# The first adjacency product of a two-layer graph kernel: begun on arriving quarters, three of its seven sub-products by an inner scheme, the transpositions and projections moved behind it

## The chip, the cores and the metric

The kernel runs on one core of one Trainium2 chip. The core has TensorE (PE; its weight loads are shown apart as PEld), VectorE (DVE), ScalarE (ACT), GpSimd (POOL) and SyncE (SP), which here only issues transfers to the core's 16 DMA engines. The metric is the device time of one execution in microseconds (us), the median over several. Everything is in 32-bit floating point.

## The reference

```
x: 16 x 1024 x 64    adj: 1024 x 1024
layer 0:  Q = x Wq' + bq;  K = x Wk' + bk;  V = x Wv'
          score = softmax(Q K', over the rows n)      # per batch, 1024 x 1024
          x = layernorm(x + (score @ adj) @ V)
layer 1:  x1 = adj @ x;  x2 = 2 adj @ x1 - x          # twice, with the same adj
          x = layernorm(x + [x, x1, x2, x1, x2] @ weight + bias)
```

The kernel multiplies adj by x first, U = adj @ x for all 16 batches at once (1024 x 1024 by 1024 x 1024), lets the softmax weights act on U, and applies Wv afterwards. Both layers together need three such products with adj: this first one, and two "hops" in layer 1.

## The kernel before

**Data.** `xs` holds x with 128 nodes on the partitions: 8 pairs of batches, 8 blocks of nodes, 128 columns (2 batches x 64). `aT` holds adj transposed, 8 blocks of 128 rows by 1024. `xT` is x with channels on the partitions (`transposed`, L104: eight 128x128 transposes into a PSUM tile, which ScalarE copies out). `GY` is x projected by one matrix made of both score weights (`project`, L127: two 128x512 matmuls, and VectorE adds the bias on the way out). `score_weight` and `score_weight_2` (L111, L118) make that matrix.

**A product with adj** (class `Product`, L245) is cut into quarters of 512 and done with seven sub-products instead of eight, named 1 to 7. It needs sums of quarters of adj (`left_sum`, S1 to S4) and of quarters of x (`right_sum`, T1 to T4), four VectorE instructions of 128x512 each; T2 and T4 overwrite T, T3 overwrites S1, and S3 overwrites a quarter of `aT`, which is loaded again later (L523). `step` (L334) is one half of a sub-product: eight 128x512 matmuls into a two-bank PSUM tile, then the read of that tile. A read of cells not touched before is a ScalarE copy; a read onto cells that hold something is a VectorE add (L308).

**The inner scheme** (`halves`, L339; `part`, L363) does one sub-product itself with seven parts of four 128x256 matmuls, 28 instead of 16 twice as wide. It takes eight more VectorE sums, four of each factor, placed in a spare buffer, and reads a 128x512 bank per part. Before the change only the two hops use it. `twice` names the sub-products that are treated so: their common term is then added where another step is read, so steps 5 and 7 are read into two places.

**Order.** The program is written out by hand and each engine follows its own order. Sums wait in a list, `line`: `later` appends, `fill(n)` issues the next n at that point of VectorE's order, `need` issues all up to a name.

**PSUM.** Of eight banks, six are three two-bank tiles that rotate (`ps_tile`), two are the accumulator (`pacc`).

**The start before** (L74 to L151). ScalarE issues the score weights' transfers, GpSimd the bias's, SP x by pairs and adj by rows of 1024, then the small weights. TensorE runs idle turns (matmuls of zeros), then interleaves eight transpositions and eight projections. Then (L491 to L528) comes the first product: all S sums and T1, `layer_weights` (small sums that prepare Wv and the second layer's weights), row sums `mu`, then all seven sub-products plain, the last half-step interleaved with the scores of two steps of the attention loop.

**The loop** (L537) has 64 steps, 8 pairs of batches by 8 blocks. In step n TensorE makes scores of step n+2 (two rotating tiles, one for each batch), then the weighted sum `acc` of step n (L437); VectorE negates the scores and takes their minimum (L407); ScalarE takes the exponentials (L414). From pair 1 on, steps also carry the layer norm, re-transposition and weights of the pair before. GpSimd subtracts the row means from `xs` (L526), which the layer norm needs in pair 1.

Of the kernel before, what the change touches and what calls it, by code (L numbers as in the profile page):

```python
# [9 lines left out]
FP = mybir.dt.float32  # L10
# [8 lines left out]
def gnn_kernel(  # L19
# [31 lines left out]
    def ps_tile(name):  # L51
        return ps.tile([P, 2 * H], FP, tag="ps", name=name)
# [18 lines left out]
    raw = const.tile([P, 5, C], FP, tag="raw", name="raw")  # L71
    w1s = const.tile([P, 5, C], FP, tag="w1s", name="w1s")
    halves = [slice(j * C, (j + 1) * C) for j in range(2)]
    for w, w_in in ((wq, wqT), (wk, wkT)):  # L74
        for s in halves:
            nc.scalar.dma_start(w[s, s], w_in)
    for s in halves:
        nc.gpsimd.dma_start(bkp[s], bk[:, None])
    for k in range(0, K8, 4):
        nc.sync.dma_start(xs[:, 0, k : k + 4], x_in[:, 0, k : k + 4])  # L80
    for p in range(1, NP):
        nc.sync.dma_start(xs[:, p], x_in[:, p])
    for k in (4, 5, 6, 7, 0, 1, 2, 3):
        nc.sync.dma_start(aT[:, k], a_in[:, k])
# [19 lines left out]
    def transposed(p, pt=None):  # L104

        pt = ps_tile("pt") if pt is None else pt
        for k in range(K8):
            nc.tensor.transpose(pt[:, ts(k, P)], xs[:, p, k, :], ident)  # L108
        nc.scalar.activation(xT[:, p], pt, AF.Copy)

    def score_weight():  # L111
        pw = ps_tile("pw")
# [3 lines left out]
        return pw  # L116

    def score_weight_2(pm):  # L118
        nc.tensor.matmul(pm[:, H : H + P], wn[:, 1], wn[:, 0], start=True, stop=True)
        nc.tensor.matmul(pm[:, 2 * H - P : 2 * H - P + 1], wn[:, 0], bkp, start=True, stop=True)  # L120
        nc.vector.tensor_copy(m_w, pm[:, H : H + P])
        nc.vector.tensor_copy(gb, pm[:, 2 * H - P : 2 * H - P + 1])

    def rows_of(p):
        return xs[:, p].rearrange("p k (b c) -> p (k b) c", b=2)

    def project(p):  # L127
        pg = ps_tile("pg")
        for h in range(2):
            nc.tensor.matmul(pg[:, ts(h, H)], m_w, xT[:, p, ts(h, H)], start=True, stop=True)  # L130
        nc.vector.tensor_scalar(GY[:, p], pg, gb, None, op0=ALU.add)

    def idle_turns(n):

        pt = pacc.tile([P, N], FP, tag="acc", name="idle")
        for _ in range(n):
            nc.tensor.matmul(pt[:, 0:P], still, still, start=True, stop=True)

    idle_turns(6)
    transposed(0)  # L140
    idle_turns(4)
    transposed(1)
    pm = score_weight()
    idle_turns(2)
    transposed(2)
    score_weight_2(pm)
    for p in range(NP):
        if p + 3 < NP:
            transposed(p + 3)
        project(p)  # L150

# [59 lines left out]
    def left_tiles():  # L211
        return {n: quarter_tile("e", f"S{n}", 3) for n in (2, 4, 1)}

# [13 lines left out]
    def by_pair(t):  # L227

        return t.rearrange("p k (q f) -> p q k f", f=P)
# [4 lines left out]
    def later(name, pieces):  # L234
        line.extend((name, piece) for piece in pieces)
# [5 lines left out]
    def need(*names):  # L241
        while any(name in names for name, _ in line):
            fill(1)

    class Product:  # L245
# [69 lines left out]
        def matmuls(self, name, g, rows=(0, 1)):  # L315
# [3 lines left out]
            for i in rows:  # L319
                for k in range(HB):  # L320
# [123 lines left out]
    def take(p):  # L444
        LN[p] = att.tile([P, N], FP, tag="rT", name="rT")
        nc.scalar.activation(LN[p], ACC.pop(p), AF.Copy)

    def norm_1(p, po=None):
# [18 lines left out]
    def weigh(p, c, pw=None):  # L467
# [20 lines left out]
            U[:, blocks, ts(p, P)].rearrange("p k (b c) -> p k b c", b=2), to[:, 1], AF.Copy  # L488
        )

    S = left_tiles()  # L491
    first = Product(
        S, xs, by_pair(U), [ps_tile("h0"), pacc.tile([P, N], FP, tag="acc", name="h1")]
        + [ps_tile(f"h{n}") for n in (2, 3)],
    )
    for n in (1, 2, 4, 3):
        later("S", left_sum(S, n))
    later("T", first.right_sum(1))
    need("S", "T")
    wv = layer_weights()  # L500
    for p in range(NP):
        nc.vector.tensor_reduce(mu[:, p], rows_of(p), AX.X, ALU.add)
    nc.vector.tensor_scalar(mu, mu, 1.0 / C, None, op0=ALU.mult)
    for name in (2, 1, 5):
        first.step(name, 0)
        first.step(name, 1)
    later("T", first.right_sum(2) + first.right_sum(3))
    need("T")
    first.step(3, 0)
    first.step(6, 0)  # L510
    first.step(6, 1)
    later("T", first.right_sum(4))
    need("T")
    first.step(7, 0)
    first.step(7, 1)
    first.step(3, 1)
    first.step(4, 0)
    for i in range(2):
        first.step(4, 1, 0, (i,))
        scores(i)  # L520
        for j in range(2):
            exponentials(i, j)
    nc.sync.dma_start(aT[:, low, right], a_in[:, low, right])  # L523
    scaled(0)
    for p in range(NP):
        nc.gpsimd.tensor_tensor(  # L526
            rows_of(p), rows_of(p), mu[:, p, :, None].to_broadcast([P, G, C]), ALU.subtract
        )  # L528


    Y = GY.rearrange("p q (k f) -> p q k f", k=K8)
# [4 lines left out]
    last = len(steps) - 1  # L536
    for n, (p, m) in enumerate(steps):  # L537
        if (p, m) == (NP - 2, 2):
            later("half", [f for both in zip(*hop_1.halves(2, room[0])) for f in both])
# [63 lines left out]
    def turns(product, room, after_5, after_6):  # L603

        S = product.S
        need("S1", "T1")
        lefts, rights = product.halves(3, room[0])
        later("half", [f for both in zip(lefts, rights) for f in both])
# [12 lines left out]
        need("S2", "T2")  # L621
        if after_5:
            later("S3", left_sum(S, 3))
        lefts, rights = product.halves(4, room[1])
        later("half", lefts)
        for g in range(2):
            product.step(6, g, 6)
            after_6(g)
        need("S3", "T3")
        later("T4", product.right_sum(4))  # L630
        later("half", rights)
        for g in range(2):
# [47 lines left out]
    later("half", [f for both in zip(lefts, rights) for f in both])  # L680
    hop_2.tiles = [h[0], h[2], h[3], h[1]]
    hop_2.step(1, 0, 9)
    hop_2.part(2, 1, two)
# [51 lines left out]
```

## Time and profile before

| quantity | value |
| --- | --- |
| time, median of 8 runs | 617.1 us (615.54 to 618.34) |
| time of the profiled execution | 617.47 us |
| its span, first to last instruction | 615.4 us |
| TensorE busy | 600.3 us (98%) |
| VectorE, ScalarE, GpSimd busy | 391.3, 225.5, 86.9 us |
| mean granted TensorE clock | 0.994 |
| first product begins, on TensorE | 32.19 us |
| weighted sum of the loop's step 0 begins | 135.74 us |
| read from HBM, written | 9.73 MB, 4.19 MB |

The profile shows one execution. A row gives start and length in us, the engine, the line of the kernel, the operation, output and inputs with their shapes, the number of instructions merged, and in brackets how long the engine had been idle and what ended that. One 32-bit matmul is two records, so counts of matmuls are twice the instructions, except for transposes. "PEclk" is the share of the full clock that TensorE was granted. In the slices each digit is a busy share in tenths.

### The profile page before, as it was taken

How to read it: one execution, taken by the hardware profiler on the slowest of the kernel's cores; microseconds unless marked ns; L12 is line 12 of the kernel's file. 1: busy time of each engine (PE TensorE's matmuls, PEld its weight loads, DVE VectorE, ACT ScalarE, POOL GpSimd, SP SyncE). 2: the span in 40 equal slices, each digit the busy share in tenths (PEclk: the TensorE clock that was granted, in tenths of full speed). 3: DMA queues.
4: the chain of work that ended last, by engine and by line, in shares of the span. 5: the costliest groups of instructions: out<-in, count | busy, mean ns of one | idle time of the engine just before them, and what ended most of it. 6: DMA issues, size and time to landing. Idle time of an engine off the chain costs nothing.

```text
span 615.4 us, 6249 instructions
## 1 busy us (share of the span) xinstructions
PE 600.3 (98%) x2414; PEld 294.3 (48%) x2414; DVE 391.3 (64%) x702; ACT 225.5 (37%) x377; POOL 86.9 (14%) x47
## 2 busy tenths in 40 slices
PE   7999999999999999999999999999999999999993
PEld 7544444433334444343444434447647466646463
DVE  0599312157776767777676787946768477558484
ACT  2300100055657767676676767662100000000111
POOL 1000004400030210303011030300000000203366
PEclk8999999999999999999999999999999999999998
DMA  7700000100000000000000000000000000000012
GB/s 289 277 0 2 0 0 0 69 0 0 2 2 0 1 0 1 2 1 1 1 0 1 1 1 1 0 1 0 2 0 1 0 0 1 0 35 35 34 70 102
DMA packets 7245, 14.32 MB, mean 23 GB/s; under 512 B 1968, under 2 KB 2992, under 8 KB 7216
## 3 DMA queue, kind: packets, MB, share of 16 engines
q1 hardware_dynamic: 6832, 13.86, 6.1%
q8 instruction: 19, 0.31, 0.2%
q10 hardware_dynamic: 320, 0.07, 0.1%
q14 instruction: 10, 0.08, 0.0%
q0 software_dynamic: 64, 0.00, 0.0%
HBM read 9.73 MB, written 4.19 MB: 23 GB/s over the span
## 4 chain that ended last, share of the span: by engine, by line
PE 92%; DVE 4%; ACT 1%; DMA 1%; issue 0%; ACTq 0%; DVEq 0%
PE h L321 33%; PE sc L400 20%; PE acc L437 19%; PE h L374 9%; PE pw L473 3%; PE po L452 2%; PE pg L130 2%; PE pt L108 2%; DMA wk<-in_wkT_dram 1%; DVE GY L308 1%; DVE U L308 1%; PE h L473 1%; DVE var L191 0%; DVE e L407 0%; DVE T L275 0%
## 5 line engine op out<-in xcount | busy, mean ns | idle before, releaser
L407 DVE TENSOR_SCALAR_CACHE_REDUCE e<-sc 128x1024 f32<-128x1024 f32 x128 | 151.6, 1222 | 64.3 <-PE sc L400 64.3
L414 ACT ACTIVATE e<-e,nm 128x1024 f32<-128x1024 f32 x128 | 146.3, 1143 | 75.3 <-DVE e L407 75.2
L400 PE MATMUL sc<-xT,GY 64*128 64x512 f32 x512 | 128.4, 615 | 0.5 <-DVE e L407 0.5
L437 PE MATMUL acc<-e,us 128*64 128x512 f32 x512 | 124.0, 605 | 0.3 <-DVE us L425 0.3
L184 POOL TENSOR_TENSOR rstd<-var,expo 128x16 f32<-128x16 f32 (+1 forms) x15 | 42.1, 2807 | 417.2 <-DVE var L179 417.2
L321 PE MATMUL h<-T,S 128*128 128x512 f32 x192 | 83.4, 592 | 0.0
L400 PEld LDWEIGHTS sc<-xT,GY 64*128 64x128 f32 x512 | 45.0, 186 | 73.4 <-issue 49.8
L308 DVE TENSOR_TENSOR U<-h,U 128x512 f32<-128x512 f32 (+1 forms) x39 | 36.1, 935 | 53.7 <-PE h L321 45.6
L437 PEld LDWEIGHTS acc<-e,us 128*64 128x64 f32 x512 | 31.0, 136 | 71.0 <-issue 60.6
L658 ACT ACTIVATE sq<-GY 128x1024 f32<-128x1024 f32 x6 | 6.3, 1058 | 147.9 <-DVE GY L308 147.9
L321 PEld LDWEIGHTS h<-T,S 128*128 128x128 f32 x192 | 36.5, 190 | 44.6 <-issue 44.2
L310 ACT ACTIVATE U<-h 128x1024 f32<-128x1024 f32 (+1 forms) x9 | 8.4, 930 | 91.4 <-PE h L321 91.4
L321 PE MATMUL h<-S,aT 128*128 128x512 f32 x96 | 41.7, 592 | 0.0
L374 PE MATMUL h<-xs 128*128 128x256 f32 x144 | 32.6, 382 | 1.4 <-DVE GY L308 1.1
L374 PEld LDWEIGHTS h<-xs 128*128 128x128 f32 x144 | 27.0, 190 | 6.2 <-DVE GY L308 1.5
L308 DVE TENSOR_TENSOR GY<-h,GY 128x512 f32<-128x512 f32 (+1 forms) x24 | 19.1, 797 | 16.7 <-PE h L321 11.2
L526 POOL TENSOR_TENSOR xs<-xs,mu 128x1024 f32<-128x1024 f32 x8 | 15.0, 1903 | 104.7 <-DVE T L275 92.3
L321 PEld LDWEIGHTS h<-S,aT 128*128 128x128 f32 x96 | 18.2, 190 | 23.0 <-issue 23.0
L321 PE MATMUL h<-xs,aT 128*128 128x512 f32 x64 | 27.6, 592 | 0.0
L473 PEld LDWEIGHTS pw<-raw,xT 64*128 64x128 f32 x224 | 19.2, 187 | 15.8 <-issue 5.8
L414 ACT ACTIVATION_READ_ACCUMULATOR e<-e,nm 128x1 f32 x128 | 24.0, 188 | 0.0
L473 PE MATMUL pw<-raw,xT 64*128 64x192 f32 x224 | 24.0, 332 | 0.0
(145 smaller groups left out, 584.0 us busy)
## 6 DMA issues: line engine op xcount, KB each, us to landing
aT<-in_adjT_dram SPq DMA_DIRECT2D x8, 512.0 KB, 10.2
xs<-in_x_dram SPq DMA_DIRECT2D x7, 512.0 KB, 7.9
out_dram<-GY SPq DMA_DIRECT2D x12, 256.0 KB, 2.3
aT<-in_adjT_dram SPq DMA_DIRECT2D x1, 1024.0 KB, 5.1
out_dram<-GY SPq DMA_DIRECT2D x8, 128.0 KB, 1.9
xs<-in_x_dram SPq DMA_DIRECT2D x2, 256.0 KB, 3.1
w1s<-in_w_dram SPq DMA_DIRECT2D x2, 80.0 KB, 9.2
wq<-in_wqT_dram ACTq DMA_DIRECT2D x2, 16.0 KB, 5.2
```

Of the source, the lines that this page charges most:

```text
L108: nc.tensor.transpose(pt[:, ts(k, P)], xs[:, p, k, :], ident)
L130: nc.tensor.matmul(pg[:, ts(h, H)], m_w, xT[:, p, ts(h, H)], start=True, stop=True)
L184: nc.gpsimd.tensor_tensor(rstd, var, expo[:, 0:g], ALU.pow)
L308: nc.vector.tensor_add(at(self.res), got, at(self.res))
L321: nc.tensor.matmul(pt[:, ts(i, H)], a[:, k, ts(2 * g + i, P)], b[:, :, k], start=(start and k == 0), stop=(k == HB - 1), skip_group_check= ...
L374: nc.tensor.matmul(pt[:, ts(i, W)], a[:, k, ts(i, P)], b[:, :, k], start=(start and i == k == 0), stop=(k == 1), skip_group_check=True,)
L400: nc.tensor.matmul(sc[j][:, ts(h, H)], GY[s, p, ts(m, P)], xT[s, p, ts(h, H)], start=True, stop=True,)
L407: nc.vector.tensor_scalar(E[n][:, j], sc[j], -1.0, None, op0=ALU.mult, op1=ALU.min, accum_out=NM[n][:, j : j + 1],)
L414: nc.scalar.activation(E[n][:, j], E[n][:, j], AF.Exp, bias=NM[n][:, j : j + 1], scale=-1.0, accum_out=SM[n][:, j : j + 1],)
L437: nc.tensor.matmul(ACC[p][j * C : (j + 1) * C, ts(h, H)], us[:, j], es[:, j, ts(h, H)], start=(m == 0), stop=(m == K8 - 1),)
L473: nc.tensor.matmul(pw[:, j, ts(k, 3 * C)], xT[s, p, ts(2 * c + k, P)], raw[s, 0:3].rearrange("p w c -> p (w c)"), start=True, stop=True,)
L526: nc.gpsimd.tensor_tensor(rows_of(p), rows_of(p), mu[:, p, :, None].to_broadcast([P, G, C]), ALU.subtract)
```

## The change

All transfers are now issued by SP. First come eight pairs: one node block of x for the first four batch pairs, and the left half of one row block of adj, 256 KB each. Then follow the other halves and the small weights.

The eight idle turns are followed at once by sub-product 1, block by block (`by_block`, new). Sub-products 2, 3 and 4 go by the inner scheme, with `GY`, which is empty as yet, as the spare buffer. In between stand the score weights, transpositions 0 to 3 and projections 0 to 3; these use the PSUM tiles of the product. Transposition 4 comes after the product, transpositions 5 to 7 and projections 4 to 7 stand in the loop's steps of pair 0. The bias of the projection is added by ScalarE. `layer_weights` comes after sub-product 7, the row sums `mu` are spread as fillers, and the means are subtracted in `centre`, five pairs before the loop and three in it.

```diff
+    for blocks in (range(K8 // 2), range(K8 // 2, K8)):
+        for k in blocks:
+            nc.sync.dma_start(xs[:, 0 : NP // 2, k], x_in[:, 0 : NP // 2, k])
+            nc.sync.dma_start(aT[:, k, 0:H], a_in[:, k, 0:H])
+    for p in range(NP // 2, NP):
+        nc.sync.dma_start(xs[:, p, 0 : K8 // 2], x_in[:, p, 0 : K8 // 2])
+    for k in range(K8):
+        nc.sync.dma_start(aT[:, k, H:N], a_in[:, k, H:N])
+    for p in range(NP // 2, NP):
+        nc.sync.dma_start(xs[:, p, K8 // 2 : K8], x_in[:, p, K8 // 2 : K8])
...
-        nc.vector.tensor_scalar(GY[:, p], pg, gb, None, op0=ALU.add)
+        nc.scalar.activation(GY[:, p], pg, AF.Identity, bias=gb, scale=1.0)
...
-    idle_turns(6)
-    transposed(0)
...
+    idle_turns(8)
...
+        def by_block(self, name):
+
+            a, b = self.factors(name)
+            for k in range(HB):
+                for i in range(HB):
+                    nc.tensor.matmul(
+                        self.tiles[i // 2][:, ts(i % 2, H)], a[:, k, ts(i, P)], b[:, :, k],
+                        start=(k == 0), stop=(k == HB - 1),
+                    )
...
+    h = [ps_tile("h0"), ps_tile("h1"), pacc.tile([P, N], FP, tag="acc", name="h2"), ps_tile("h3")]
+    two = h[2:]
+    first = Product(S, xs, by_pair(U), h, None, (2, 3, 4))
+    room = [GY[:, 4 * z : 4 * z + 4].rearrange("p q n -> p (q n)") for z in range(2)]
+    first.by_block(1)
+    later("half", both(*first.halves(2, room[1])))
+    need("half")
+    for g in range(2):
+        first.read(1, g)
+    later("T1", first.right_sum(1))
+    for n in (1, 2, 4):
+        later(f"S{n}", left_sum(S, n))
+    for q in PARTS:
+        first.part(2, q, two, {1: 0, 5: 2, 7: 2}.get(q, 1))
+    need("T1", "S1")
+    first.step(5, 0, 8)
+    need("S4")
+    later("half", both(*first.halves(3, room[0])))
+    first.step(5, 1, 8)
+    need("half")
+    later("T2", first.right_sum(2))
+    later("T3", first.right_sum(3))
+    later("S3", left_sum(S, 3))
+    for q in PARTS:
+        first.part(3, q, two)
+    score_weight(h[3])
+    need("T2")
+    lefts, rights = first.halves(4, room[1])
+    later("half", lefts)
+    later("mu", [
+        lambda p=p: nc.vector.tensor_reduce(mu[:, p], rows_of(p), AX.X, ALU.add)
+        for p in range(NP)
+    ])
+    first.step(6, 0, 5)
+    transposed(0, h[2])
+    score_weight_2(h[3])
+    first.step(6, 1, 6)
+    transposed(1, h[2])
+    project(0, h[3])
+    need("S3", "T3")
+    line[:0] = [("T4", f) for f in first.right_sum(4)]
+    first.step(7, 0, 6)
+    transposed(2, h[2])
+    project(1, h[3])
+    transposed(3, h[2])
+    line[:0] = [("half", f) for f in rights]
+    first.step(7, 1, 6)
     wv = layer_weights()
+    project(2, h[2])
+    project(3, h[3])
+    need("T4", "half")
+    for q in PARTS:
+        first.part(4, q, two)
+        if q == 6:
+            scores(0)
+            for j in range(2):
+                exponentials(0, j)
+    need("mu")
...
+    scores(1)
+    for j in range(2):
+        exponentials(1, j)
+    transposed(4)
     scaled(0)
+    for p in range(5):
+        centre(p)
...
+        elif p == 0 and m:
+            if m in (1, 3, 5):
+                transposed(m // 2 + 5)
+                centre(m // 2 + 5)
+            else:
+                project((m + 1) // 2 + 3)
```

`both` interleaves the sums of the two factors. The order within a sub-product's parts is 1, 2, 6, 5, 7, 3, 4.

More of the change, by code (lines that the diff above doesn't have):

```diff
@@ L73, in gnn_kernel @@
     halves = [slice(j * C, (j + 1) * C) for j in range(2)]
+    for blocks in (range(K8 // 2), range(K8 // 2, K8)):
[8 more added lines that the diff above has]
+        nc.sync.dma_start(xs[:, p, K8 // 2 : K8], x_in[:, p, K8 // 2 : K8])
     for w, w_in in ((wq, wqT), (wk, wkT)):
         for s in halves:
-            nc.scalar.dma_start(w[s, s], w_in)
+            nc.sync.dma_start(w[s, s], w_in)
     for s in halves:
[L78 to L84, printed above, removed]
+        nc.sync.dma_start(bkp[s], bk[:, None])
     for s in halves:
@@ L109, in transposed, with score_weight @@
         nc.scalar.activation(xT[:, p], pt, AF.Copy)
-    def score_weight():
-        pw = ps_tile("pw")
+    def score_weight(pw):
         nc.tensor.transpose(pw[:, 0:P], wq, ident)
@@ L115, in score_weight, with project @@
         nc.vector.tensor_copy(wn, pw[:, 0 : 2 * P].rearrange("p (a o) -> p a o", a=2))
-        return pw
     def score_weight_2(pm):
[L119 to L122, printed above, removed]
+        nc.tensor.matmul(pm[:, 0:P], wn[:, 1], wn[:, 0], start=True, stop=True)
+        nc.tensor.matmul(pm[:, H : H + 1], wn[:, 0], bkp, start=True, stop=True)
+        nc.vector.tensor_copy(m_w, pm[:, 0:P])
+        nc.vector.tensor_copy(gb, pm[:, H : H + 1])
     def rows_of(p):
         return xs[:, p].rearrange("p k (b c) -> p (k b) c", b=2)
-    def project(p):
-        pg = ps_tile("pg")
+    def project(p, pg=None):
+        pg = ps_tile("pg") if pg is None else pg
         for h in range(2):
             nc.tensor.matmul(pg[:, ts(h, H)], m_w, xT[:, p, ts(h, H)], start=True, stop=True)
-        nc.vector.tensor_scalar(GY[:, p], pg, gb, None, op0=ALU.add)
+        nc.scalar.activation(GY[:, p], pg, AF.Identity, bias=gb, scale=1.0)
     def idle_turns(n):
@@ L137, in idle_turns @@
             nc.tensor.matmul(pt[:, 0:P], still, still, start=True, stop=True)
-    idle_turns(6)
-    transposed(0)
[L141 to L150, printed above, removed]
+    idle_turns(8)
     def layer_weights():
@@ L446, in take, with centre @@
         nc.scalar.activation(LN[p], ACC.pop(p), AF.Copy)
+    def centre(p):
+        nc.gpsimd.tensor_tensor(
+            rows_of(p), rows_of(p), mu[:, p, :, None].to_broadcast([P, G, C]), ALU.subtract
+        )
     def norm_1(p, po=None):
@@ L489, in weigh, with both @@
         )
+    def both(lefts, rights):
+        return [f for pieces in zip(lefts, rights) for f in pieces]
     S = left_tiles()
[L492 to L499, printed above, removed]
-    wv = layer_weights()
-    for p in range(NP):
-        nc.vector.tensor_reduce(mu[:, p], rows_of(p), AX.X, ALU.add)
@@ L503, in gnn_kernel @@
-    nc.vector.tensor_scalar(mu, mu, 1.0 / C, None, op0=ALU.mult)
[L504 to L522, printed above, removed]
+    h = [ps_tile("h0"), ps_tile("h1"), pacc.tile([P, N], FP, tag="acc", name="h2"), ps_tile("h3")]
@@ L523, in gnn_kernel @@
+    need("mu")
+    nc.vector.tensor_scalar(mu, mu, 1.0 / C, None, op0=ALU.mult)
     nc.sync.dma_start(aT[:, low, right], a_in[:, low, right])
+    scores(1)
+    for j in range(2):
+        exponentials(1, j)
+    transposed(4)
     scaled(0)
[L525 to L528, printed above, removed]
+    for p in range(5):
+        centre(p)
     Y = GY.rearrange("p q (k f) -> p q k f", k=K8)
@@ L538, in gnn_kernel @@
         if (p, m) == (NP - 2, 2):
-            later("half", [f for both in zip(*hop_1.halves(2, room[0])) for f in both])
+            later("half", both(*hop_1.halves(2, room[0])))
         if n + 2 <= last:
@@ L607, in turns @@
         lefts, rights = product.halves(3, room[0])
-        later("half", [f for both in zip(lefts, rights) for f in both])
+        later("half", both(lefts, rights))
         for g in range(2):
@@ L679, in gnn_kernel @@
     lefts, rights = hop_2.halves(2, room[0])
-    later("half", [f for both in zip(lefts, rights) for f in both])
+    later("half", both(lefts, rights))
     hop_2.tiles = [h[0], h[2], h[3], h[1]]
```

## The prediction

> **What bounds the kernel now.** First the page: share of each engine, then the 40 slices.
>
> ```profile
> span 615.4 us, 6249 instructions
> ...
> PE 600.3 (98%) x2414; PEld 294.3 (48%) x2414; DVE 391.3 (64%) x702; ACT 225.5 (37%) x377; POOL 86.9 (14%) x47
> ...
> PE   7999999999999999999999999999999999999993
> ```
>
> TensorE is the bound from the second slice to the last but one, so a microsecond of TensorE work or waiting taken out there is a microsecond of the span; only slice one has holes. Next the chain that ended last, in order of time, shows what sets the start:
>
> ```profile
> 3.04 7.45 DMA wk<-in_wkT_dram
> 25.48 6.87 PE pg L130 x16
> 32.35 92.70 PE h L321 x216
> 125.05 1.92 PE sc L400 x8
> ```
>
> The first product (L321) runs without a hole from 32.2, behind the projections (L130). Its row counts are halves of instructions: a 128x512 matmul is two rows of 0.429 us, 0.858 us. A plain product of 16 is 13.73 us. The timeline of TensorE and the windows of the load show how the first 32 us go:
>
> ```profile
> 1.06 2.93 PE L137 MATMUL idle<-still 128*128 128x128 f32 x12 [1.06 <-DVE still L66]
> ...
> 9.06 1.10 PE L108 MATMUL pt<-ident,xs 128*128 128x128 f32 x8 [1.67 <-DMA xs<-in_x_dram]
> ...
> 25.32 7.03 PE L130 MATMUL pg<-xT,m_w 128*128 128x512 f32 x16
> 32.19 27.63 PE L321 MATMUL h<-xs,aT 128*128 128x512 f32 x64
> ```
>
> ```profile
> 2.00:4.00 2.00, 1.00 0.95 296
> ...
> 10.00:12.00 2.00, 0.63 1.04 424
> ...
> 26.00:28.00 2.00, 1.00 0.32 65
> ```
>
> Columns of the second: length, granted clock, DMA share, GB/s. The load keeps the 16 engines full at 410 GB/s from 8 to 26 and ends near 27; TensorE does idle turns, transposes and projections meanwhile. The useful part of that is 8 transposes x 0.88 (repeat of pt+pg at 16.66, 19.26: 2.59, less 1.72) + 8 projections x 1.72 (2 matmuls) + 0.7 for the score weights = 21.5 us. About 10.7 us of the first 32.2 are therefore waste.
>
> What an inner-scheme part costs is seen where the hops already use it (timeline around 504):
>
> ```profile
> 504.15 5.45 PE L374 MATMUL h<-xs 128*128 128x256 f32 x24 [0.19 <-DVE U L308]
> 504.62 0.68 DVE L308 TENSOR_TENSOR U<-h,U 128x512 f32<-128x512 f32 x1
> ```
>
> Four 128x256 matmuls are 8 rows of 0.215, 1.72 us; 28 (56 rows in the chain) are 12.02-12.09. Each read is 0.69 on VectorE, starting 0.2 after the matmuls end; each half-sum is 0.69 too; in a row they start 0.60 apart (four S rows in 2.49).
>
> **The skill.** *DMA: Bandwidth & Descriptors*, "Why small descriptors are slow", gives bytes/32+3 cycles a piece. The trace's packet medians (18 ns for 256 B, 46 for 1,024, 84 for 2,048, 160 for 4,096) agree up to some 5 ns more; for the new 512-byte pieces of x, which no run shows, I take 27 ns, an estimate between 18 and 46 on the line of the others. The same page, "Latency and other measured facts", reports a two- to fourfold loss of rate for HBM rows at large power-of-two pitches; no run here shows it, and it is my upper bound. *TensorE: Matmul & The Clock Gate*, "Part 1", says that the clock is half until a free-running window of some 3.4 us was busy; the trace agrees (clock 0.50 from 10.5 to 13.9, after the 1.67 us gap; the early 128x128 idle turns take 0.47). *ScalarE: Activation LUTs*, "What ACT_TABLE_LOAD costs", puts a per-partition bias at 93 ns; the trace's copy is 1.02 and its exponential with such a bias 1.15, so the projection's move from VectorE (1.28) to ScalarE is taken at 1.12.
>
> **The change, along the profiled clock.** P1 to P7 are the seven products.
>
> Load. The queue first issues 8 pairs of 256 KB (x piece, adj piece), then 1 MB of x, 2 MB of adj, 1 MB of x, weights. The first 256 KB issued at 0.74 landed 3.0 later; with 512-byte pieces (512 x 27/16 = 0.87 against 0.67) it lands at 4.0 and its adj partner at 4.7. A pair takes 0.87+0.67 = 1.54, so all eight end at 1.9+12.3, landing near 15.3; x's next at 18, adj's right half at 23.4, the rest at 26. The queue keeps eight transfers open (2 MB, 6 us of moving), so its waits do not starve the engines; an issue takes 0.33-0.43.
>
> P1 starts at 4.8, behind eight idle turns (1.06+3.4 = 4.5) and the first pair. Cold until about 7 (as before): +1.05. It needs a pair each 3.43 us and gets one each 1.54, so ends at 19.6. VectorE's eight half-sums (4.9 us) run 15.3-20.2, before the first read at 21.5: hidden, with 2 us to spare.
>
> P2 (inner, 12.02) ends at 31.6. Each of its seven parts leaves VectorE 1.72 us for a read (0.69) and one or two sums (0.6) queued ahead of it, which fits: x's 1 MB is there from 18, adj's right half from 23.4, its first sum (S1) is due at 27.5. At the end it doesn't fit: the sixth part ends at 29.9, its read runs 30.1-30.8, the last S1 sum to 31.4, the seventh part's read 31.8-32.5, and P5 writes that very bank: wait 0.95. P5 (13.73) ends at 46.2; S2, S4 and P3's half-sums (16 x 0.6 = 9.7) run inside it. P5's results are read twice by ScalarE (2 x 1.02); P3's second part wants the second tile, free 2.3 after P5, but is ready after 1.72: wait 0.6. P3 ends at 58.9. Then score weights (0.25) and P6 (13.73) in halves, with transposes 0 and 1 (2 x 0.88), score_weight_2 (0.45) and projection 0 (1.72) between: to 76.8. After P7's first half (6.87, to 83.7) ScalarE's copy of the block waits for VectorE's add of the same tile (0.2+1.22+0.1, then 1.02); the copy of transpose 2 (1.02) stands behind it, and transpose 3 needs that tile: 3.6 after the half, against 2.6 of TensorE work (transpose 2, projection 1): wait 1.0. P7's second half, projections 2 and 3 (3.44), wait 0.3 for their ScalarE copies; layer_weights (45.6 to 48.5 in the trace, 2.9 us) and the remaining means stand in VectorE's queue here, ahead of P4's first read, but end 0.2 before that is due. P4 and scores(0): to 112.8. scores(1), then transpose 4, which takes the third PSUM buffer, so that scores(2) wait for both minima instead of one: 1.1 more than the 1.4 of before, transpose 4 lying inside it. Score sums of step 0 then start at 119.2, against 135.74.
>
> The same as a ledger, in us: start of the product 32.2 to 4.8, -27.4; three inner products 3 x (13.73-12.02), -5.1; cold +1.05; four transposes inside the product +3.5, three in pair 0's steps at 1.02 (as at 221.1) +3.1; eight projections +13.7; score weights +0.7; waits 0.95+0.6+1.0+0.3+1.1 = +3.95. Sum -6.5.
>
> In pair 0's steps the additions are pure TensorE time: a step is 3.78 (1.92+1.87), ScalarE's two exponentials plus a copy or projection are 3.8 against 4.8 or 5.5, VectorE's 2.9 fit, and the extra PSUM tile is read 1.0 before its next use. If that cover failed, up to 1 us in each of seven steps. POOL's centring moves after the means and has eight steps before norm_1 wants it: nothing. The small weights leave ScalarE's and POOL's queues (2.4 and 1.2 us of issuing) for the end of SP's, land between 28 and 40 (eleven, whose issues stood up to 1.28 apart) and are used from 59: nothing; if they were late, score_weight would stop TensorE. The reload of adj's quarter moves with P7 and is wanted 300 us later: nothing. All code from pair 1 on is the same.
>
> 617.47 - 6.5 = 611.0 for the profiled execution (span 615.4 plus 2.1 around it); on the median of 617.1, **610.6**.
>
> **Rivals.** *A, the ledger* (0.64): 609 to 612.5. Low end: P2 to P4 wait less (-1.5); high: the clock turns full one window later (+1.7).
>
> *B, part given back* (0.19): the 512-byte pieces cost 40 to 55 ns, or VectorE's in-order reads wait a little in each of 21 parts. At 45 ns the load of the eight pairs is 4096 x 18/16 = 4.6 longer, less 2 spare: +2.6; 0.1 us a part gives +2. So 612.5 to 616. For it: the queue of VectorE is dense in P2; against: the hops' 144 rows of the same kind show 1.4 us of idle in all.
>
> *C, slower* (0.10): those pieces are all at one offset in 4 KB rows; if HBM serves them at a third of the rate (80 ns), the pairs end 13.6 later, and P2's part three, which waits for its first part's read behind all half-sums, starts 11.6 late: 622. It decides from 27 + (6.5+2) x 16/4096 = 60 ns on. Against it: x in 4 KB pieces and adj moved at over 400 GB/s, and the late half-row reload of adj (1 MB) landed in 5.1.
>
> *D, no change to be measured* (0.05): the pieces near 56 to 64 ns, 616 to 618.
>
> *E, the change doesn't do what it says* (0.02): P1 does not start before all eight pairs have landed, at 15.3: +10.5, so 621. The first transposes, begun at 3.87 when the first two transfers had landed, speak against it.
>
> **How the numbers follow.** No change means within 0.2% (1.2 us), about what this kernel's measurement can tell. A and B are faster: 0.83; D the same: 0.05; C and E slower: 0.12. The range runs from 608.5 to 616, A and B together; A's own is 609 to 612.5.
>
> **What would show it.** First product at 4.8 and P1's rows without holes; part one of P2 at 19.6; half-sums of P2 done by 20.2; waits near 32, 47, 88 and 116 of 0.6 to 1.1; acc's first row near 119; the pair-0 loop 10 us longer. Wrong if the eight pairs land after 17.5, if TensorE's holes before 119 pass 6 us, or if pair 0's steps exceed 3.78 + 1.0 or 1.72.

## The result, and the profile after

| quantity | before | after | predicted |
| --- | --- | --- | --- |
| time, median (us) | 617.38 (614.9 to 619.13, 32 runs) | 611.86 (611.4 to 612.52, 11 runs) | 610.6 |
| profiled execution, its span (us) | 617.47, 615.4 | 611.75, 610.0 | 611.0, 608.9 |
| first product begins (us) | 32.19 | 4.98 | 4.8 |
| weighted sum of step 0 begins (us) | 135.74 | 119.42 | 119.2 |

The ratio of the times is 0.9912, 95% interval 0.9900 to 0.9925. The gain is 5.5 us where 6.5 were forecast; 611.86 lies in the range of 608.5 to 616 and in that of case A, the ledger (609 to 612.5). The runs of the kernel before lie in two groups, 7 of the 32 at 614.9 to 615.9 and the others at 616.7 to 619.1, so that beside its fastest runs the gain is 3 to 4 us.

First the page of the changed kernel, as it was read for the kernel before: shares of the engines and the 40 slices.

```profile
span 610.0 us, 6448 instructions
...
PE 594.0 (97%) x2478; PEld 303.2 (50%) x2478; DVE 408.2 (67%) x737; ACT 232.9 (38%) x384; POOL 85.8 (14%) x45
...
PE   8999999999999999999999999999999999999993
```

TensorE is still the bound from the second slice to the last but one. Its busy time fell by 6.3 us and VectorE's rose by 17, the direction in which the inner scheme exchanges one for the other. Next the chain that ended last, in order of time (start, length, what):

```profile
4.84 7.01 DMA xs<-in_x_dram
11.87 6.09 DMA xs<-in_x_dram
...
22.95 8.91 PE h L375 x40
31.89 0.70 DVE U L299
32.63 14.02 PE h L312 x32
```

In the kernel before, the chain came in through the score weights' transfer and the projections. Now it comes in through the load of the eight pairs and VectorE's sums of them, and joins TensorE only at 22.95, inside sub-product 2. (The transfer at 11.87 is the one issued after the eight pairs; the view infers releasers, and VectorE's first row below shows the wait that counts, for the last piece of adj.) Product 1 lies beside the load and is not on the chain: with this landing it could have ended some 0.7 later at no cost, and what sets the pace is when the eighth pair lands.

The timeline of TensorE shows the marks that the prediction named (start, length, instruction, count; in brackets the idle time before the row and what ended it):

```profile
4.98 13.97 PE L322 MATMUL h<-xs,aT 128*128 128x512 f32 x32 [0.53 <-DMA aT<-in_adjT_dram]
18.79 3.62 PE L375 MATMUL h<-xs,aT 128*128 128x256 f32 x16
22.95 5.45 PE L375 MATMUL h<-GY 128*128 128x256 f32 x24 [0.55 <-DVE U L299]
...
32.63 14.00 PE L312 MATMUL h<-T,S 128*128 128x512 f32 x32 [0.78 <-DVE U L299]
...
87.31 1.09 PE L112 MATMUL h<-ident,xs 128*128 128x128 f32 x8 [0.70 <-ACT xT L113]
...
116.36 3.12 PE L401 MATMUL sc<-xT,GY 64*128 64x512 f32 x8 [0.29 <-DVE e L408]
119.42 1.94 PE L438 MATMUL acc<-e,us 128*64 128x512 f32 x8
...
128.01 1.98 PE L132 MATMUL pg<-xT,m_w 128*128 128x512 f32 x4
129.92 1.94 PE L438 MATMUL acc<-e,us 128*64 128x512 f32 x8
```

Four things are to be seen. Product 1 starts when the first pair is there, 0.53 after TensorE was ready, and its 32 rows take 13.97, as the 32 of product 5 at 32.63 do (14.00): nothing of it ran at half clock in this execution. The third part of product 2 waited at 22.95, which the prediction did not have. The waits at 32.6 and 87.3 are forecast ones. The brackets count from the modelled end of the row before, so they are some 0.17 short; from start to start, less the work, the three are 0.72 (22.95 - 18.79 - 2 x 1.72), 0.95 and 0.85. And in the loop the projection begun at 128.01 puts the next row 1.91 later (129.92), not 1.72. The row of length 3.12 at 116.36 (scores of step 2, behind transposition 4) holds the rest of the wait for the PSUM tiles: it is 1.1 longer than the usual 1.99.

The load, in windows of 2 us (length, busy time and count of PE, PEld, DVE, ACT, POOL, then granted clock, DMA share, GB/s), and the first and last of VectorE's work on the eight pairs:

```profile
2.00:4.00 2.00, 2.00 (x12) 2.00 (x11) 0.00 (x0) 0.01 (x1) 0.00 (x0) 1.00 0.84 257
4.00:6.00 2.00, 1.47 (x7) 0.83 (x7) 0.00 (x0) 0.00 (x0) 0.00 (x0) 1.00 0.90 233
6.00:8.00 2.00, 2.00 (x6) 0.86 (x5) 0.00 (x0) 0.00 (x0) 0.00 (x0) 1.00 1.00 315
8.00:10.00 2.00, 2.00 (x6) 0.95 (x5) 0.00 (x0) 0.00 (x0) 0.00 (x0) 1.00 1.11 343
...
26.00:28.00 2.00, 2.00 (x11) 1.76 (x10) 2.00 (x5) 0.00 (x0) 0.00 (x0) 1.00 0.48 138
```

```profile
17.39 0.69 DVE L356 TENSOR_TENSOR GY<-aT 128x512 f32<-128x512 f32 x1 [16.08 <-DMA aT<-in_adjT_dram]
...
22.21 0.68 DVE L299 TENSOR_TENSOR U<-h,U 128x512 f32<-128x512 f32 x1
...
99.39 1.22 DVE L531 TENSOR_REDUCE mu<-xs 128x16 f32<-128x1024 f32 x1
100.75 0.69 DVE L299 TENSOR_TENSOR U<-h,U 128x512 f32<-128x512 f32 x1
```

From 8 to 16 the load moves at 332 to 344 GB/s; two transfers of 262,144 bytes in the assumed 1.54 us are 340. But from 2 to 8 the rate was only 257, 233 and 315, and the half-sums began at 17.39 instead of 15.3 and ended at 22.2 instead of 20.2. By the landings in the trace the first pair was there at 4.84 and the second only 2.99 later, at 7.83; the other six followed 1.52 to 1.60 apart, the last at 17.27. (The clock column shows 1.00 until the first change that the trace records, so what was granted in the first us is read from the lengths of rows.) The median packet of 512 bytes took 27 ns, the estimate. At 100.75 stands the first read of product 4. `layer_weights` (96.45 to 99.4) and one row sum, which end at 100.61, stand ahead of it and did not hold it up.

### The profile page after: what moved, and what is told of

Read it like the earlier page. It is cut to its first block, busy times and chain, and to the rows that moved or that the text cites. A ratio compares the mean times of both kernels' runs of the same rounds, so it can differ in the third digit from the quotient of the medians.

```text
span 610.0 us, 6448 instructions
## 1 busy us (share of the span) xinstructions
PE 594.0 (97%) x2478; PEld 303.2 (50%) x2478; DVE 408.2 (67%) x737; ACT 232.9 (38%) x384; POOL 85.8 (14%) x45
## 4 chain that ended last, share of the span: by engine, by line
PE 89%; DVE 5%; DMA 2%; ACT 2%; SPq 1%; issue 1%; DVEq 0%; ACTq 0%
PE h L312 24%; PE sc L401 20%; PE acc L438 19%; PE h L375 15%; PE pw L479 3%; PE po L458 2%; DMA xs<-in_x_dram 2%; PE pt L112 2%; PE pg L132 1%; DVE U L299 1%; PE h L132 1%; DVE GY L299 1%; PE h L479 1%; ACT U L301 0%; PE h L112 0%
## 5 line engine op out<-in xcount | busy, mean ns | idle before, releaser
L299 DVE TENSOR_TENSOR U<-h,U 128x512 f32<-128x512 f32 (+1 forms) x58 | 48.2, 836 | 50.1 <-PE h L312 30.3
L375 PE MATMUL h<-xs 128*128 128x256 f32 x144 | 32.6, 382 | 1.4 <-DVE GY L299 1.1
L301 ACT ACTIVATE U<-h 128x1024 f32<-128x1024 f32 x8 | 8.0, 1022 | 54.8 <-PE h L312 24.7
L490 DVE TENSOR_TENSOR xT<-pw,raw 128x256 f32<-128x256 f32 x28 | 11.9, 425 | 18.7 <-ACT GY L489 18.7
```

The costliest lines, as they stand in the source:

```text
L299: nc.vector.tensor_add(at(self.res), got, at(self.res))
L375: nc.tensor.matmul(pt[:, ts(i, W)], a[:, k, ts(i, P)], b[:, :, k], start=(start and i == k == 0), stop=(k == 1), skip_group_check=True,)
```

## The experiments

Two theories were open for the missing microsecond, and one for the whole. *Loop*: projections and transpositions (128x128) put between the scores (64x128) and weighted sums (128x64) of pair 0 cost more than their own length. *Queue*: the inner scheme's sums and reads, in order on VectorE, give back part of what the seven parts save. *Clock*: part of the gain, and the steadier times, are half-clock windows that no longer occur. Each kernel is a variant of the changed one unless it says otherwise.

**Product 2 plain.**

```diff
-    later("half", both(*first.halves(2, room[1])))
-    need("half")
...
-    for q in PARTS:
-        first.part(2, q, two, {1: 0, 5: 2, 7: 2}.get(q, 1))
+    for g in range(2):
+        first.step(2, g, 4)
```

> The changed kernel with sub-product 2 done plainly (two half-steps of 13.73 us in all instead of seven parts of 12.02), everything else as changed. Theory (the waits around the inner scheme are real time on the path): in the changed kernel sub-product 2 costs 12.02 plus a wait of 0.55 before its third part and of 0.78 before sub-product 5, 13.35 in all; both waits go, so +0.4 us: 612.2. Rival 1 (the waits are only displaced and the inner scheme gives its full 1.7 us): 613.6. Rival 2 (the inner scheme's VectorE load costs more than its matmuls save): faster than the changed kernel, 611 or less.

Measured: 611.46 us (611.04 to 611.83), ratio 0.9900 (0.9875 to 0.9924). TensorE's timeline:

```profile
19.07 13.90 PE L312 MATMUL h<-xs,aT 128*128 128x512 f32 x32
32.81 1.45 PE L312 MATMUL h<-T,S 128*128 128x512 f32 x3
```

The plain product takes 32.81 - 19.07 = 13.74 without a hole; the inner one took 32.63 - 18.79 = 13.84: seven parts of 1.72, and 1.80 of waits (0.72 for the half-sums, 0.95 for the last read, 0.13 between). At this place, where the factors have only just landed, the inner scheme is worth nothing: it saves 1.7 and waits 1.8. (The spans of the two traces are 610.1 and 610.0; the 0.4 between the medians is too little to rank the two kernels.)

**All three plain.** As above for 2, 3 and 4, with the tiles of the kernel before; the scores of step 0 stand between the two rows of product 4's second step.

```diff
-    first = Product(S, xs, by_pair(U), h, None, (2, 3, 4))
+    first = Product(S, xs, by_pair(U), h)
...
-    for q in PARTS:
-        first.part(3, q, two)
+    first.step(3, 0, 4)
+    first.step(3, 1, 4)
...
+    first.step(4, 0, 1)
+    first.step(4, 1, 1, (0,))
```

> The changed kernel with sub-products 2, 3 and 4 all plain: only the early start, the spread transpositions and projections, and the new loads remain. Theory: matmul time +3 x 1.72 = +5.1, waits of 0.55, 0.78 and 0.30 go, so +3.5 us: 615.4, which leaves the early start a gain of about 2 against the kernel before. Rival (the early start gives nearly the whole gain and the inner scheme little): 612 to 613. Rival (the early start gives nothing by itself, its added waits eat it): 617 or more.

Measured: 614.49 us (613.95 to 615.83), ratio 0.9960 (0.9941 to 0.9979); the weighted sum of step 0 began at 121.96, 2.54 later than in the changed kernel. The variant has a wait of its own, as `score_weight` takes the tile that product 3's read still holds (ScalarE, 59.99 to 61.01; the profile itself names no releaser):

```profile
61.11 0.30 PE L116 MATMUL h<-ident,wq 128*128 128x128 f32 x1 [1.16 <-issue]
```

So the inner scheme is worth 2.6 us at most, and some 1.3 with that wait taken off, of the 5.1 in the ledger. Most of the rest is returned as waits, from start to start: 1.80 in product 2, 0.47 in product 3, and 0.85 before transposition 3, which this variant's trace does not have. The early start, with everything else, is worth 617.75 - 614.49 = 3.3 us by the medians. Between the traced executions it is 2.9, and 1.8 of that is a slow start of the kernel before in its trace, as its busy variant shows below.

**The pairs later.** The x pieces of the eight pairs go as two transfers of 256-byte pieces each (lines after L76 are one higher in its rows).

```diff
-            nc.sync.dma_start(xs[:, 0 : NP // 2, k], x_in[:, 0 : NP // 2, k])
+            for s in halves:
+                nc.sync.dma_start(xs[:, 0 : NP // 2, k, s], x_in[:, 0 : NP // 2, k, s])
```

> The changed kernel with each 256 KB piece of x for the first four batch pairs fetched as two transfers of 256-byte pieces (18 ns each in the trace of before) instead of one of 512-byte pieces (27 ns). The eight pairs then take 8 x (1024 x 18 - 512 x 27)/16 ns = 2.3 us longer. Theory (VectorE's half-sums for sub-product 2 start when the last pair has landed, and sub-product 2's third part waits for them): the wait of 0.55 grows to 2.9 and the start of the first matmul slips 0.3; +2.3 to +2.6 us: 614.3. Rival (the load is hidden behind sub-product 1): within 0.5 of the changed kernel, 612.2.

Measured: 613.55 us (612.78 to 615.78), ratio 0.9942 (0.9921 to 0.9963). TensorE's timeline, and a window of it:

```profile
24.87 7.13 PE L376 MATMUL h<-GY 128*128 128x256 f32 x24 [2.14 <-DVE U L300]
```

```profile
26.00:28.00 2.00, 2.00 (x6) 1.55 (x5) 0.77 (x3) 0.00 (x0) 0.00 (x0) 0.50 1.04 376
```

The half-sums began at 19.31, 1.92 later than in the changed kernel, product 1 began and ended 0.32 later, and the wait in product 2 grew by the difference, from 0.55 to 2.14: once the pairs are late, their landing sets this stage one for one. Something was added that nobody had put in the sum: after the wait the same 24 rows took 7.13 instead of 5.45, because the clock was half for one window. The seven runs spread over 3 us, four of them at 612.8 to 613.6, two at 614.7 and one at 615.8.

**Fewer waits.** The order around four waits is changed, and no work. Four of product 2's half-sums come ahead of its parts and the others between them; product 5's second step goes first, so that ScalarE frees the tile which product 3 wants next, and product 3 uses its two banks in turned order; transposition 3 goes behind the matmuls of product 7's second step.

```diff
-    need("half")
+    fill(4)
...
-        first.part(2, q, two, {1: 0, 5: 2, 7: 2}.get(q, 1))
+        first.part(2, q, two, {1: 0, 3: 4, 4: 0}.get(q, 2))
...
-    first.step(5, 0, 8)
+    first.step(5, 1, 8)
...
-    first.step(5, 1, 8)
+    first.step(5, 0, 8)
...
-        first.part(3, q, two)
+        first.part(3, q, two[::-1])
...
-    transposed(3, h[2])
     line[:0] = [("half", f) for f in rights]
-    first.step(7, 1, 6)
+    first.matmuls(7, 1)
+    transposed(3, h[3])
+    fill(6)
+    first.read(7, 1)
```

> The changed kernel with the same work in another order: only four of sub-product 2's half-sums stand ahead of its first read on VectorE, the others among its parts; sub-product 5 begins with its second half, whose PSUM tile is free earlier; sub-product 3 and the transpositions use the two spare tiles the other way round; transposition 3 comes after the second half of sub-product 7, with VectorE's read of that half issued behind it. Theory (three of the waits seen, 0.55, 0.78 and 0.70, are avoidable and on the path): -2.0 to -2.2 us: 609.7. Rival (VectorE's queue in sub-product 2 is full, so the wait returns before sub-product 5): -0.7 to -1.0: 611.0.

Measured: 610.06 us (609.71 to 610.63), ratio 0.9877 (0.9853 to 0.9901). The waits of TensorE up to 170 us, the first one aside (line, what it waited for, total, times, longest):

```profile
PE h L312 <- DVE U L299: 0.7, 1, 0.7
PE h L375 <- ACT U L301: 0.3, 1, 0.3
PE sc L401 <- DVE e L408: 0.3, 1, 0.3
PE h L322 <- DMA aT<-in_adjT_dram: 0.3, 1, 0.3
```

Gone are the 0.55 in product 2 and the 0.70 before transposition 3; acc of step 0 began at 117.50, 1.92 earlier, and the median is 1.80 under the changed kernel's 611.86. The wait before product 5 stayed, because four S1 sums stood in VectorE's order ahead of the last reads. The 0.3 in product 3 stayed too, and product 1, begun at 4.58, waited 0.3 for a pair. The two waits that went were a matter of order, not of the amount of VectorE's work.

**One block.** The transpositions 5 to 7 and projections 4 to 7 leave the loop's steps of pair 0 and stand in one block before its first scores.

```diff
     for j in range(2):
         exponentials(1, j)
     transposed(4)
+    transposed(5)
     scaled(0)
...
+    project(4)
+    transposed(6)
+    project(5)
+    transposed(7)
+    project(6)
+    project(7)
...
-        elif p == 0 and m:
-            if m in (1, 3, 5):
-                transposed(m // 2 + 5)
-                centre(m // 2 + 5)
-            else:
-                project((m + 1) // 2 + 3)
```

> The changed kernel with transpositions 5 to 7 and projections 4 to 7 taken out of pair 0's steps and done in one block behind transposition 4, ahead of scores(2), with transpositions 4 and 5 copied by ScalarE ahead of the exponentials of step 1. Theory (in the steps each projection costs 1.91 instead of 1.72 and each transposition 1.02 instead of 0.88, because they stand between matmuls on half the rows; in one block they cost the small price, and the wait of scores(2) for both minima, 1.4 us, is covered): -0.19 x 4 - 0.14 x 3 = -1.2, the wait's -1.4 given back in part by ScalarE's copies in the block, so -1.0 to -2.0: 610.4. Rival (the block is bound by ScalarE's and PSUM's turns, seven reads of 1.0 to 1.1 behind two exponentials): 612 to 613.

The changed kernel itself was run beside it as the base:

> The changed kernel once more, unedited, on the chip and beside the runs of before that the other three of this set share: 611.9 (611.4 to 612.5), against which they are read.

Measured: the base 612.01 us (611.68 to 612.18), ratio 0.9912 (0.9887 to 0.9938); one block 610.25 us (609.73 to 610.61), ratio 0.9884 (0.9862 to 0.9907). TensorE's timeline:

```profile
122.47 3.79 PE L132 MATMUL pg<-xT,m_w 128*128 128x512 f32 x8
...
128.11 1.94 PE L438 MATMUL acc<-e,us 128*64 128x512 f32 x8
129.98 1.99 PE L401 MATMUL sc<-xT,GY 64*128 64x512 f32 x8
...
160.26 2.05 PE L458 MATMUL po<-wv,rT 128*128 128x128 f32 x16
```

With the same instructions gathered the kernel is 1.76 us faster. Pair 0's work ends (row `po`) at 160.26 instead of 162.29. The loop up to there takes 32.15, as it did in the kernel before, against 42.87 in the changed kernel; and the block costs 8.69 more before it, against 10.7 in the steps. Where the 2.0 are: the seven instructions' work is 10.2 in the block (between two of its kind a projection is 1.72 and a transposition 0.87, but entering and leaving the block costs some 0.7 with a short wait) against 10.7 in the steps; 1.1 is the wait inside the row of step 2's scores, which the block covers; and 0.4 fell away before the block, in product 2, because the pairs landed that much earlier in this execution (first half-sum at 17.00), which is not the edit's doing. So the edit is worth 1.6 in the traces: 0.5 by the shapes, 1.1 by the covered wait.

**Both edits**, with one more of the first kind: two S1 sums go behind product 2's last reads.

```diff
-        first.part(2, q, two, {1: 0, 5: 2, 7: 2}.get(q, 1))
+        first.part(2, q, two, {1: 0, 4: 1}.get(q, 2))
```

> The edits of fewer_waits and of one_block together, and in sub-product 2 two of the sums S1 moved behind the reads of its last two parts on VectorE. In fewer_waits sub-product 5 still waited 0.71 us for those reads. Theory (that wait goes too, and the gains add): 610.1 - 0.7 - 1.5 = 607.9. Rival (the waits share a cause and only one edit counts): 609.5 or more.

Measured: 607.59 us (607.0 to 608.17), ratio 0.9842 (0.9817 to 0.9868), the fastest of all. The waits of TensorE up to 170 us, the first one aside:

```profile
PE h L375 <- ACT U L301: 0.3, 1, 0.3
PE pt L112 <- DVE e L408: 0.3, 1, 0.3
```

The gains add up: 4.4 us from the base, of which the two single edits give 3.6 and the wait before product 5 the rest. From product 1's start to 170 us TensorE now waits 0.6 us in all.

**The bias back on VectorE.** One part of the change undone, which the prediction had priced at nothing.

```diff
-        nc.scalar.activation(GY[:, p], pg, AF.Identity, bias=gb, scale=1.0)
+        nc.vector.tensor_scalar(GY[:, p], pg, gb, None, op0=ALU.add)
```

> The changed kernel with one part of the change undone: the projection's bias is added by VectorE again instead of ScalarE. The prediction priced this part at next to nothing (1.12 against 1.28 us, both off the path). Reading of the changed kernel's queues: VectorE is not free everywhere. Projections 2 and 3 stand behind layer_weights (to 99.4) in VectorE's order, so their reads would run 99.4 to 102, while product 4's first parts want those two PSUM tiles from about 99.1 and 100.8: waits of about 1.6 and 0.8, +2.4 us together. In the loop's steps of pair 0 VectorE has 2.9 us of work in steps of 5.7, so nothing there. Expected 614.3, between 613.3 and 615.5. If the engine of the bias doesn't matter, as the prediction's price said: 611.8 to 612.3. If the in-order minima behind the projection hold up the loop too, 1 us more in each of four steps: 617 or more.

Measured: 614.50 us (613.49 to 615.65), ratio 0.9953 (0.9934 to 0.9972). VectorE's rows of projections 2 and 3, TensorE's row behind them, and a window there:

```profile
99.02 2.48 DVE L133 TENSOR_SCALAR GY<-h,gb 128x1024 f32<-128x1024 f32 x2
```

```profile
100.36 5.41 PE L375 MATMUL h<-T,aT 128*128 128x256 f32 x16 [2.04 <-DVE GY L133]
```

```profile
102.00:103.80 1.80, 1.80 (x5) 1.44 (x5) 0.70 (x2) 0.00 (x0) 0.00 (x0) 0.50 0.00 0
```

The two projections stand behind `layer_weights` in VectorE's order, and product 4 waits for them: one wait of 2.04, where 1.6 and 0.8 were expected. In the loop nothing came of it. So the move to ScalarE is worth 2.6 us here at the medians, not for the 0.16 between the two instructions, but because it takes them out from behind 2.9 us of other work. And again a wait of 2 us brought a half-clock window: 16 rows took 5.41 instead of 3.72, and the runs lie in two groups, four at 613.5 to 613.9 and four at 615.2 to 615.7, 1.7 apart. The traced run is of the upper group; if the lower one had no such window, which no trace shows, the wait alone is worth about 1.8 and the rest is the clock.

**The kernel before, kept busy.** Not a variant of the changed kernel: the two later groups of idle turns in the kernel before are made longer, to fill the gap after which its clock was half.

```diff
     transposed(0)
-    idle_turns(4)
+    idle_turns(10)
     transposed(1)
     pm = score_weight()
-    idle_turns(2)
+    idle_turns(4)
```

> The kernel before with eight more idle turns (ten instead of four behind transposition 0, four instead of two behind the score weights' transposes), so that TensorE does not fall idle for 1.67 us while it waits for x. Theory (the kernel before loses time, and scatters over 614.9 to 620.2, because that gap puts TensorE on the half clock for 3.4 us in a varying place; the changed kernel is busy from 1.05 on and so has lost the penalty with the gap): no half-clock stretch after the first 8 us, the runs lie within 2 us of each other, and the median is 0.5 to 2 us lower: 616.0. Rival (the half clock at the start is hidden behind the loading of x, and the scatter comes from the loads or from later): 617.4 and the same scatter of some 5 us.

Measured: 616.84 us (615.62 to 619.26), ratio 0.9999 (0.9980 to 1.0018). In the profiled execution (span 613.6) the window at half clock is gone and the first product begins 1.87 earlier than in the kernel before:

```profile
30.32 15.18 PE L321 MATMUL h<-xs,aT 128*128 128x512 f32 x35
```

But the scatter stays: 7 of the 14 runs lie at 617.2 to 619.3. The ratio shows no gain; that the median is 616.84 against the 617.87 of the kernel before beside it says little, as it falls between two groups of runs. The theory *Clock*, that this one gap is what separates the runs of the kernel before, is not borne out. Where its slower executions lose their time was not seen, since each trace shows one.

What the two traces differ in is seen, though. The 1.87 is the whole difference between their spans, 615.4 and 613.6. The transfer of the second score weight let TensorE go on at 9.90 instead of 10.63, and from there to the first projection it took 3.18 instead of 4.32, with two more idle turns but at full clock: 0.73 and 1.14. Against 613.6 the changed kernel's trace gains 3.6 us, not 5.4, and the trace with all three plain gains 1.1. About a third of the gain between the traced executions is thus a slow start in the one execution of the kernel before, which the prediction's ledger took as the rule.

## Why the prediction was right, and where it was off

**The start.** Right: 4.98 for 4.8, so a gain of 27.2 instead of 27.4. But 1.87 of it is the slow start of the one execution of the kernel before on which the ledger was built; the trace of its busy variant reaches the first product at 30.32.

**The cold clock, +1.05.** This differed from one execution to the next. In the trace above product 1 had no row at half clock and ended at 18.79 instead of 19.6. In the trace of the same kernel run as the base of one block its first rows took 1.03 to 1.19 instead of 0.59, and it ended at 19.66, as forecast:

```profile
4.93 14.89 PE L322 MATMUL h<-xs,aT 128*128 128x512 f32 x32
19.66 3.62 PE L375 MATMUL h<-xs,aT 128*128 128x256 f32 x16
...
33.05 14.00 PE L312 MATMUL h<-T,S 128*128 128x512 f32 x32 [0.78 <-DVE U L299]
```

The difference of 0.87 did not reach product 5. There the half-sums began at 17.80, and product 5 15.25 later; in the trace above it is 17.39 and 15.24, in the traces of one block and of the bias on VectorE 17.00 and 17.01, and 15.24. With the pairs as late as they came, the landing sets this path, and the term is not on it.

**The landing of the pairs.** Wrong by 2 us: half-sums to 22.2 instead of 20.2. The price of a piece (27 ns) was right, and so was the pace from the second pair on (1.52 to 1.60 against 1.54). The step that failed is the beginning: the sum let the pairs follow at full rate from the first one, and the second came 2.99 after it. Why was not tried. The 2 us that the forecast had to spare took this up almost exactly, so product 5 began at 32.63, forecast 32.55, but by another path: the sum came there through product 1 and the cold clock, the trace through the landing and a wait of 0.72 in product 2. That the two agree is luck; a landing 0.4 later, in the second trace, gave 33.05.

**The inner products, -5.1.** The size of 12.02 without waits holds, and most of the waits were named in a term of their own. Taken with them the scheme is worth 1.3 to 2.6 us, and nothing in product 2.

**The waits, +3.95.** From start to start: before product 5 0.95 (forecast 0.95), in product 3 0.47 (0.6), before transposition 3 0.85 (1.0), around product 4 some 0.3 in small pieces (0.3), and from the end of step 1's scores to the weighted sum of step 0 4.45, less 1.92 for a step's scores 2.53 with transposition 4 inside (forecast 1.4 + 1.1). The places were right, and what was waited for. `layer_weights` and the means were done about a tenth of a us before product 4's first read; the run with the bias on VectorE shows what stands behind this cover: 2 us, and the clock.

**The loop of pair 0, +9.94.** Here is most of the microsecond that was missing. From the weighted sum of step 0 to the first row of `po` it is 42.87 against 32.2, so +10.7. The transpositions cost 1.02, as taken from a later step of the loop; the projections were taken at 1.72, the price between rows of 128, and cost 1.91 between the loop's scores and weighted sums. Four times 0.19 is 0.76. The step that was mis-sized is thus "four projections x 1.72". In the gathered block a projection between two transpositions takes 1.72 again (119.88 to 121.60). The trace has it in the means too: 16 projection records among the loop's average 618 ns, the 16 in the product 592. The prediction's own sign of being wrong, steps over 3.78 + 1.72, came true by 0.2: a step with a projection is 5.70 (124.22 to 129.92). Another, pairs landing after 17.5, was missed by 0.2 in this trace (17.27) and met in the second one (17.68).

**The sum.** -16.3 up to step 0 (forecast -16.5), +10.7 in pair 0 (forecast +9.9), +0.2 in the rest of the run (forecast none): -5.4 in the profiled span. That the part up to step 0 fits to 0.2 rests on the luck above.

**The rivals.** B's mechanism, dense queues on VectorE, was there in the 0.95 before product 5, which A's sum had, and in tenths elsewhere. Its other part, dear pieces, was not: 27 ns. The 0.72 in product 2 came by the path that C describes, a first read behind half-sums that began late. C and D needed 56 ns or more. That the lateness of the pairs would decide is shown by the run with 256-byte pieces: 1.92 later at the half-sums cost 1.7 at the median. E is excluded by the start at 4.98.

The Trainium skill's prices held where they were used. *DMA: Bandwidth & Descriptors*, "Why small descriptors are slow": its bytes/32+3 cycles ranks the pieces rightly, and the 27 ns measured lie on the line of the trace's own medians. *ScalarE: Activation LUTs*, "What ACT_TABLE_LOAD costs", has 93 ns for the bias; the projection's read takes 1.12 against 1.02 for the copy.

## What to carry to other kernels

Work that is hidden beside a load is free only until the first instruction that needs all of the load: find that one, and put the orders of the other engines so that its predecessors come first. When a scheme trades a slower engine's instructions for the bound's, price it with the waits of its reads in order, and try leaving it out where its inputs have just landed. Move filler instructions into one block of their own shape rather than between matmuls of other shapes, above all where the block also covers a wait, and look at what stands ahead of an instruction in its engine's queue before deciding which engine takes it. A ledger built on one traced execution takes that execution's start for the rule: read a second trace before pricing what it shows.

## What was not expected of the hardware

A wait of some 2 us on TensorE, with full work on both sides, can cost 1.7 us more than itself: after waits of 2.14 and 2.04 us the clock was half for 3.4 us in the traces, and the runs of one of these kernels lie in two groups 1.7 apart. In the kernel before such a window followed waits of 1.67 and 0.37 close together. Steps of the clock lie multiples of 3.41 us apart in these traces, and in the 3.41 ahead of each of the three windows TensorE stood for 1.9 to 2.1. Waits of 0.3 to 0.8, and one of 1.16 (all three plain), had no such window after them. The Trainium skill (*TensorE: Matmul & The Clock Gate*, "What's actually happening" in Part 1) puts the return to half clock after an idle window of about 3.4 us, so by these runs less idle time than a whole window is enough.

When the full clock first comes also varies: the kernel before and its busy variant begin with the same instructions, and their second group of idle turns ran at half clock in one and at full clock in the other, 0.22 and 0.12 us a row:

```profile
5.61 1.78 PE L137 MATMUL idle<-still 128*128 128x128 f32 x8
```

```profile
4.83 2.40 PE L137 MATMUL idle<-still 128*128 128x128 f32 x20
```

A group of 128x128 matmuls between the loop's scores (64x128) and weighted sums (128x64) takes 0.15 (the eight of a transposition: 1.02 against 0.87) to 0.19 us (the two of a projection: 1.91 against 1.72) more than among its own kind, and in the gathered block the last two projections, before scores, take 3.72 instead of 3.44: the price seems to lie at the change of shape. What in TensorE takes this time was not tried.
